# State-space step of a conv-attention hybrid: another order of its parts, split projections, masks on GpSimd

## The chip, the cores and the metric

The kernel runs on one core of a Trainium2 chip. All times are device microseconds (us) of that core; lower is better. Of the unchanged kernel three runs are given: 3096.25 us median, 3092.15 lowest, 3098.95 highest. One more execution was recorded by the hardware profiler; it took 3095.44 us, and its span from the first to the last instruction is 3093.7 us.

## What is computed

The input is four images of 128 channels and 64 x 64 pixels. A first layer (normalisation, convolutions, attention) is followed by a second one: a state-space block and a recurrence over the 4096 tokens of each image. The change lies in the state-space block, which runs once forward and once backward over the tokens. Cut to what matters:

```python
zxbcdt = x @ in_proj                                  # x: (b, 4096, 128), after a layer norm
z, xbc, dt = split(zxbcdt)
xbc = silu(causal_conv4(xbc) + conv_b)                # four taps along the tokens
xh, Bm, Cm = split(xbc)                               # 4 heads of 64, state of 64
dt = softplus(dt + dt_bias);  A = -exp(A_log)
# per chunk: Acs = cumsum(dt * A); L = exp(Acs[l] - Acs[s]) for s <= l, else 0
Y_diag = einsum('bcln,bcsn,bchls,bcshp->bclhp', Cc, Bc, L, xc)
states = einsum('bcln,bclh,bclhp->bchpn', Bc, decay_st, xc)
new    = st + carry * dec                             # the scan over chunks
Y_off  = einsum('bcln,bchpn,bclh->bclhp', Cc, prev, exp(Acs))
y  = Y_diag + Y_off + xh * D
yg = y * silu(z)
yn = yg * rsqrt(mean(yg * yg) + eps) * norm_w
return yn @ out_proj                                  # forward + reversed backward
```

All values are float32. The kernel takes chunks of 128 tokens where the reference takes 64; the result is the same function.

## The kernel before

`mamba` holds the stage. A *sequence* is one image: 32 *steps* of 128 tokens (`NT`), in eight *groups* of four steps (`NG`, `MT`). A step handles both directions at once: partitions 0 to 63 carry the forward state, 64 to 127 the backward one (`HALF`). In all there are 128 steps and 32 groups.

*The projections of a group*, for 512 columns each: `project_bc` (B or C of both directions, four taps each, two half-array products side by side, L1109), `project_fwd` (four taps, L1121), `project` (one product L1130, then ScalarE's identity with the last tap L1135, and three taps on VectorE L1141), `project_z` (L1152, Silu L1153), `outputs` (L1314). Their PSUM tiles come from `ring`, a pool of three banks, tag "big". The row statistics of other sequences (L83 to L89), which run in between, use the same ring.

*A step.* `load` fetches by DMA the cumulated decays of the chunk, spread over all partitions: `lt` (L1160, three buffers) and `ct` (L1164, two buffers). `differences` forms max(0, cs - row) for each head on ScalarE (L1174). `prepare` transposes B (`p_bt`, L1193), forms the products of B and C (`p_g`, L1195), takes Exp of the whole `lt` (L1197), copies B (L1199), weights the tokens with dt and dtd (L1202), zeroes `p_g` outside the triangle (`gm`, L1206), multiplies it into `lt` (L1207) and C into `ct` on GpSimd (L1208). `turn` transposes the tokens (L1183). `states` multiplies tokens and B (`p_st`, L1218), lets the carried state fade on GpSimd (L1227) and adds (L1230). `scan` forms y from `lt` (L1240) and from the carried state and `ct` (L1248). `take` adds the D term after every second step (L1260). `p_g`, `p_bt` and `p_st` are parts of one PSUM tile, `small`, of two banks.

*The end of a group.* `gate` multiplies with z on GpSimd (L1273), `squares` squares and adds (L1279, L1282), `means` takes the mean over channels by a product with 32 columns (L1289), adds epsilon (L1293), sends the row through DRAM into columns, takes the power -1/2 on GpSimd (L74) and spreads it back by DMA (`rs`). `back` multiplies by `rs` (L1352) and adds to the residual stream (L1355).

*Order.* Inside the stage TensorE and ScalarE run in the order of the code (`manual_schedule`); VectorE, GpSimd and SyncE, which issues the DMAs, are put in order by a scheduler from priorities and estimated times. The main loop over n does, in this order: open step n+2, states(n), turn(n+1), scan(n), prepare(n+1), take, the work of a position j = n mod 4, differences(n+2), and pieces of the opening of the next sequence and the ending of the last one. By j: 0 squares, px, pb for B, px; 1 means, px, pb for C; 2 `project_fwd`, three `activate`, all four pz, gate; 3 gate, back.

Of the kernel before, what the change touches and what calls it, by code (L numbers as in the profile page):

```python
# [16 lines left out]
P = 128  # L17
# [876 lines left out]
def mamba(nc, tc, k, a, t, B, T, vec, first=None, after=None, mr=None):  # L894
# [16 lines left out]
    with ExitStack() as ctx:  # L911
# [29 lines left out]
        mean = wp.tile([P, QT], F32, name="mean")  # L941
# [53 lines left out]
        engines = (mybir.EngineType.PE, mybir.EngineType.Activation)  # L995
        ctx.enter_context(tc.manual_schedule(engines=set(engines)))
        small = ps.tile([P, 2, NC], F32, name="small")
        p_g, p_bt, p_st = small[:, :, 0:P], small[:, 0, P : 2 * P], small[:, 1, P : P + DI]
# [5 lines left out]
        def steps(b, tl):  # L1004
# [72 lines left out]
            nc.vector.tensor_copy(flat(cs), pcs[:, 0])  # L1077
# [7 lines left out]
            pr = p_g if b == 0 else ring.tile([P, ND, P], F32, tag="big", name="pr")  # L1085
# [4 lines left out]
            nc.scalar.activation(row[:, 1], pr, AF.Exp)  # L1090
# [25 lines left out]
        def project_fwd(gr):  # L1116

            tl, g = gr["tl"], gr["at"][1]
            px = ring.tile([P, MG], F32, tag="big", name="px")
            for tap in range(KC):  # L1120
                nc.tensor.matmul(px, w[0]["x"][:, tap, :], tl[:, rows(g, 0, tap)], start=(tap == 0), stop=(tap == KC - 1))  # L1121
            nc.scalar.activation(gr["x"][0][:, 0, :], px, AF.Silu, bias=w[0]["cb"][:, 0:1])

        def project(gr, i, c):
# [5 lines left out]
            nc.tensor.matmul(px, wx, tl[:, rows(g, i, PAD)], start=True, stop=True)  # L1130
# [16 lines left out]
        def project_z(gr, i, c):  # L1147
# [4 lines left out]
            nc.tensor.matmul(pz, w[i]["z"][:, bass.ts(c, P)], tl[:, rows(g, i, PAD)], start=True, stop=True)  # L1152
            nc.scalar.activation(gr["z"][i][:, c, :], pz, AF.Silu)  # L1153

        def load(m):
# [6 lines left out]
            m["ct"] = wk.tile([P, NHEAD, P], F32, tag="ct", name="ct")  # L1162
# [6 lines left out]
        def differences(m):  # L1169

            for d in range(ND):
                for h in range(NHEAD):
                    v = m["lt"][:, d, h, :]
                    nc.scalar.activation(v, v, AF.Relu, scale=-1.0, bias=m["b"]["cs"][:, d, m["i"], h : h + 1])  # L1174

        def turn(m):
# [4 lines left out]
            for d in range(ND):  # L1181
                for c in range(2):
# [3 lines left out]
                    )  # L1186

        def prepare(m):

            gr, i = m["g"], m["i"]  # L1190
            Bs, Cs = gr["bc"][0], gr["bc"][1]
            cols = bass.ts(i % MT, P)
            nc.tensor.transpose(p_bt, Bs[:, cols], k.ident)  # L1193
            for d in range(ND):
                nc.tensor.matmul(p_g[:, d, :], Bs[HALF[d], cols], Cs[HALF[d], cols], start=True, stop=True)  # L1195
            lt = m["lt"]
            nc.scalar.activation(lt, lt, AF.Exp, scale=-1.0)  # L1197
            m["bt"] = wk.tile([P, P], F32, tag="bt", name="bt")
            nc.scalar.copy(m["bt"], p_bt)  # L1199
            for name in ("dt", "dtd"):  # L1200
                m[name] = wk.tile([P, ND, NHEAD, HD], F32, tag="x" + name, name="x" + name)
                nc.vector.tensor_tensor(  # L1202
                    m[name], m["xh"], m["b"][name][:, :, i, :].unsqueeze(3).to_broadcast([P, ND, NHEAD, HD]), ALU.mult
                )
            gm = wk.tile([P, ND, P], F32, tag="gm", name="gm")
            nc.vector.tensor_tensor(gm, p_g, k.tri, ALU.mult)  # L1206
            nc.vector.tensor_tensor(lt, lt, gm.unsqueeze(2).to_broadcast([P, ND, NHEAD, P]), ALU.mult)  # L1207
            nc.gpsimd.tensor_tensor(  # L1208
                m["ct"], m["ct"], Cs[:, cols].unsqueeze(1).to_broadcast([P, NHEAD, P]), ALU.mult
            )  # L1210

        def states(m, S):

# [8 lines left out]
            S1 = wk.tile([P, NHEAD, HD], F32, tag="S", name="S1")  # L1222
            st = p_st.rearrange("p (h c) -> p h c", c=HD)
            if S is None:
                nc.vector.tensor_copy(S1, st)
            else:
                nc.gpsimd.tensor_tensor(  # L1227
                    S1, S, m["b"]["tot"][:, i, :].unsqueeze(2).to_broadcast([P, NHEAD, HD]), ALU.mult
                )
# [3 lines left out]
        def scan(m, y, S):  # L1233

            i = m["i"]
            at = [bass.ts(i % 2, P), bass.ts(1 - i % 2, P)]
            for c in range(2):
                for d in range(ND):
                    for h in range(2):
# [3 lines left out]
                        )  # L1243
            if S is not None:
# [8 lines left out]
        def take(gr, j, y):  # L1253

            for d in range(ND):
                cols = half(d, j // 2)
                v = grp.tile([P, 2, 2 * P], F32, tag=f"y{d}", name=f"yT{d}", bufs=3)
# [11 lines left out]
        def gate(gr, j, split=False):  # L1269
            for d in range(ND):  # L1270
# [13 lines left out]
        def means(gr):  # L1284


            pm = ring.tile([ND * QT, MG], F32, tag="big", name="pm")
            for d in range(ND):
                nc.tensor.matmul(  # L1289
                    pm[bass.ts(d, QT)], mean, gr["z"][d][:, 0, :], start=True, stop=True, tile_position=(0, d * QT)  # L1290
                )
            ms = wk.tile([ND * QT, MG], F32, tag="row", name="ms", bufs=3)
# [3 lines left out]
            nc.sync.dma_start(m1.rearrange("(d q) n -> d (q n)", d=ND), ms[::QT])  # L1296
            col = wk.tile([P, n], F32, tag="col", name="col")
            nc.sync.dma_start(col, m1)
# [11 lines left out]
        def outputs(gr, d):  # L1310
            po = ring.tile([P, MG], F32, tag="big", name="po")
            for i in range(2):
                for c in range(2):
                    nc.tensor.matmul(  # L1314
                        po[:, half(d, i)], w[d]["out"][:, c, :], gr["y"][d][i][:, c, :],
                        start=(c == 0), stop=(c == 1),
                    )
# [90 lines left out]
        differences(m[0])  # L1408
        for i, c in STEPS_X:
            activate(groups[0], i, c)  # L1410
        turn(m[0])
        prepare(m[0])
        differences(m[1])
        S, y = None, None
        for n in range(N):
# [3 lines left out]
            last = g == NG - 1  # L1419
            if n + 2 < N:  # L1420
                open_step(n + 2)
            if n % NT == 0:
                S = None
            S1 = states(m[n], S)
            if n + 1 < N:
                turn(m[n + 1])
            if n % 2 == 0:
# [335 lines left out]
```

## Time and profile before

| | |
|---|---|
| runs, median (range) | 3096.25 us (3092.15 to 3098.95) |
| profiled execution, time and span | 3095.44 us, 3093.7 us |
| mean granted TensorE clock | 0.973 |
| busy share PE, DVE, ACT, POOL | 92%, 73%, 59%, 59% |
| convolution and attention, 0 to 1570 us | 1570 us |
| preparation of the state-space stage, 1570 to 1650 us | 80 us |
| state-space stage, 1650 to 2960 us | 1310 us |
| recurrence, 2960 to 3094 us | 134 us |

PE is TensorE, PEld its weight loads, DVE is VectorE, ACT ScalarE, POOL GpSimd, SP SyncE. A float32 product shows as two matmul instructions, a transpose as one. The stages are stretches of the span, told apart by the lines that run in them. The busy time of PE is an upper bound of its work, since matmuls overlap and their ends are modelled; the start of one matmul to the start of the next is the better measure of what it costs. An idle time is put down to the event that came last before the engine went on.

Some durations of the stage, each the mean of one instruction in the profile:

| line | what | ns |
|---|---|---|
| L1174 | ACT Relu of 128 x 128 (eight in a row take 2.43 us) | 390 |
| L1197 | ACT Exp of 128 x 1024 | 1057 |
| L1197, L1113, L1122 | ACT table load | 1283 |
| L1206 | DVE triangle, 128 x 256 | 416 |
| L1207 | DVE `lt` times `gm`, 128 x 1024 | 1393 |
| L1202 | DVE tokens times dt, 128 x 512, from PSUM | 684 |
| L1141 | DVE one tap, 128 x 512 | 748 |
| L1260 | DVE D term, 128 x 256 | 471 |
| L1208 | POOL `ct` times C, 128 x 512 | 1328 |
| L1273 | POOL gate, 128 x 512 | 1351 |
| L48 | POOL select, 128 x 128 (made once, in the beginning) | 300 |

### The profile page before, as it was taken

What the parts mean: (1) busy time and instruction counts of PE and PEld (TensorE: products, weight loads), DVE (VectorE), ACT (ScalarE), POOL (GpSimd) and SP (SyncE); (2) the same over time, 40 slices, a digit from 0 to 9 for tenths busy, and PEclk for the clock granted to TensorE, in tenths of its full rate; (3) what the DMA queues carried; (4) which work ended last, traced back from release to release, by engine and by line L of the source; (5) the groups of instructions that cost most, each with busy time, mean ns of one, the idle gap of its engine ahead of it and who ended that gap; (6) DMA issues with size and microseconds to landing.
All of it is one profiled execution on the core that took longest, in us unless ns stands there. A gap on an engine that the chain in (4) does not pass through costs nothing. (4 is left out here: it accounts for less than half of the span.)

```text
span 3093.7 us, 51126 instructions
## 1 busy us (share of the span) xinstructions
PE 2858.4 (92%) x19607; PEld 1461.9 (47%) x19607; DVE 2245.6 (73%) x3461; ACT 1834.4 (59%) x3134; POOL 1812.9 (59%) x1393
## 2 busy tenths in 40 slices
PE   6799999999999999999997999998999999999886
PEld 2345444454444554444463444444544444555455
DVE  6886677777787767788865767676777767676667
ACT  3253445444454444444526878876888778888756
POOL 4167458557585575876652565566556565555644
PEclk9899999999999999999998999999999999999988
DMA  5310011010100101011023343433333343333332
GB/s 185 136 39 31 24 47 34 21 44 24 47 32 23 44 24 47 28 50 44 16 81 92 90 124 86 109 88 113 96 96 92 91 103 97 100 102 101 83 111 111
DMA packets 108426, 224.68 MB, mean 73 GB/s; under 512 B 25678, under 2 KB 29390, under 8 KB 106764
## 3 DMA queue, kind: packets, MB, share of 16 engines
q1 hardware_dynamic: 96588, 177.53, 19.8%
q10 hardware_dynamic: 11584, 43.78, 4.2%
q8 instruction: 157, 2.57, 0.4%
q14 instruction: 97, 0.79, 0.1%
HBM read 200.83 MB, written 20.44 MB: 72 GB/s over the span
## 5 line engine op out<-in xcount | busy, mean ns | idle before, releaser
L480 DVE TENSOR_TENSOR es<-es,ex 128x1024 f32<-128x1024 f32 x448 | 703.0, 1569 | 83.6 <-ACT ex L463 43.2
L463 ACT ACTIVATE ex<-pf 128x1024 f32<-128x1024 f32 x512 | 497.8, 1021 | 403.8 <-PE pf L461 365.0
L461 PE MATMUL pf<-theta,phi 64*64 64x512 f32 x4096 | 496.7, 599 | 19.2 <-ACT ex L463 18.8
L473 PE MATMUL acc<-ex,gT 64*64 64x512 f32 x4096 | 486.7, 596 | 7.9 <-ACT ex L463 7.9
L1208 POOL TENSOR_TENSOR ct<-ct,Cst 128x512 f32<-128x512 f32 x128 | 170.0, 1328 | 344.0 <-DMA ct<-csmem 304.8
L1174 ACT ACTIVATE lt<-lt,cs 128x128 f32<-128x128 f32 x1024 | 312.1, 390 | 0.4 <-DMA lt<-csmem 0.4
L367 PE MATMUL pm<-yf,wt 128*128 128x256 f32 x1152 | 287.6, 382 | 15.9 <-DVE es L486 11.5
L473 PEld LDWEIGHTS acc<-ex,gT 64*64 64x64 f32 x4096 | 158.5, 135 | 298.2 <-issue 286.5
L461 PEld LDWEIGHTS pf<-theta,phi 64*64 64x64 f32 x4096 | 147.3, 133 | 311.7 <-issue 212.7
L367 PEld LDWEIGHTS pm<-yf,wt 128*128 128x128 f32 x1152 | 212.6, 189 | 99.2 <-issue 43.5
L410 ACT ACTIVATE eo<-pm 128x256 f32<-128x256 f32 x88 | 33.8, 384 | 367.6 <-PE pm L367 367.6
L1109 PE MATMUL pb<-tl,wbc_fwd 128*64 128x512 f32 x512 | 240.9, 614 | 6.9 <-DVE xT L1141 6.9
L1109 PE MATMUL pb<-tl,wbc_bwd 128*64 128x512 f32 x512 | 241.5, 615 | 0.0
L337 POOL TENSOR_TENSOR yf<-yd 128x272 f32<-128x272 f32 x192 | 230.4, 1228 | 1.4
L1273 POOL TENSOR_TENSOR yT<-yT,zT 128x512 f32<-128x512 f32 x127 | 170.9, 1351 | 57.2 <-DVE yT L1260 49.9
L1207 DVE TENSOR_TENSOR lt<-lt,gm 128x1024 f32<-128x1024 f32 x128 | 178.3, 1393 | 1.9
L337 POOL TENSOR_TENSOR yf<-xp 128x272 f32<-128x272 f32 x128 | 119.0, 961 | 97.4 <-PE pm L367 91.6
L1141 DVE SCALAR_TENSOR_TENSOR xT<-px,taps_bwd,xT 128x512 f32<-128x512 f32 x192 | 143.6, 748 | 9.7 <-ACT xT L1135 5.1
L1109 PEld LDWEIGHTS pb<-tl,wbc_fwd 128*64 128x64 f32 x512 | 66.6, 140 | 173.9 <-issue 142.1
L1240 PE MATMUL y<-lt,xdt 128*64 128x128 f32 x2048 | 141.2, 280 | 6.9 <-PE ptr L1183 4.2
L367 PE MATMUL pm<-yf,wc 128*128 128x256 f32 x512 | 133.4, 389 | 14.8 <-DVE eo L414 8.2
L1227 POOL TENSOR_TENSOR S<-S,tot 128x256 f32<-128x256 f32 x120 | 89.6, 746 | 96.1 <-PE y L1248 85.2
(299 smaller groups left out, 5714.9 us busy)
## 6 DMA issues: line engine op xcount, KB each, us to landing
lt<-csmem SPq DMA_DIRECT2D x128, 512.0 KB, 5.5
wt<-wd ACTq DMA_DIRECT2D x72, 576.0 KB, 3.7
ct<-csmem SPq DMA_DIRECT2D x256, 128.0 KB, 5.2
rs<-m SPq DMA_DIRECT2D x31, 512.0 KB, 3.7
wd<-t SPq DMA_DIRECT2D x16, 576.0 KB, 2.8
t<-in_x SPq DMA_DIRECT2D x4, 2048.0 KB, 10.7
rows<-after SPq DMA_DIRECT2D x32, 256.0 KB, 5.2
out<-t SPq DMA_DIRECT2D x4, 2048.0 KB, 14.3
```

The source lines that it names most:

```text
L337: nc.gpsimd.tensor_tensor(f[:, kx], at(x), at(y), op)
L367: nc.tensor.matmul(pm[:, e, :], wt, src, start=(i == 0), stop=(i == len(terms) - 1))
L461: nc.tensor.matmul(pf[c, e, :], phi[HALF[e], m, c], th[HALF[e]], start=True, stop=True)
L463: nc.scalar.activation(ex, pf, AF.Exp, scale=scale)
L473: nc.tensor.matmul(acc[r][HALF[e]], gT[HALF[r], 2 * m + e, :], ex[HALF[r], e, :], start=(m == 0), stop=(m == NT // 2 - 1),)
L480: nc.vector.tensor_tensor(es, es, ex, ALU.add)
L1109: nc.tensor.matmul(out, w[i]["bc"][:, tap, bass.ts(c, DS)], src, start=(tap == 0), stop=(tap == KC - 1),)
L1141: nc.vector.scalar_tensor_tensor(at(n), px, taps[:, PAD - n : KC - n], at(n), ALU.mult, ALU.add)
L1174: nc.scalar.activation(v, v, AF.Relu, scale=-1.0, bias=m["b"]["cs"][:, d, m["i"], h : h + 1])
L1207: nc.vector.tensor_tensor(lt, lt, gm.unsqueeze(2).to_broadcast([P, ND, NHEAD, P]), ALU.mult)
L1208: nc.gpsimd.tensor_tensor(m["ct"], m["ct"], Cs[:, cols].unsqueeze(1).to_broadcast([P, NHEAD, P]), ALU.mult)
L1273: eng.tensor_tensor(v, v, gr["z"][d][:, :, half(d, j // 2)], ALU.mult)
```

## The change

The parts of a step are cut anew and put in another order:

- The mask moves. `mask` puts 1e30 into `lt` outside the triangle, on GpSimd, ahead of the exponential; `gm` and its product with the triangle are gone, and `weigh` multiplies `lt` by `p_g` straight from PSUM. The cumulated sums are stored negated, and `decays` takes one Exp for each head in place of Relu, with no Exp of the whole tile after it.
- VectorE joins the engines that run in the order of the code. GpSimd and SyncE stay with the scheduler.
- `product` issues a projection as two halves of 64 output columns; `project_fwd`, `project`, `project_z` and `outputs` use it. The products of B and C (`likeness`) are four of 64 x 64 in place of two of 64 x 128, the means use 64 columns in place of 32.
- The transpose of B goes to a tile of the ring and follows the transposes of the tokens in `turn`.
- In a step: states, scan, carried state, load of step n+3, mask(n+2), `reads` and `fade` (n+1), likeness and weigh (n+1), turn and tokens (n+1), take, pieces of other sequences, work of j, decays(n+2). For at = 4 to 11 the opening's piece stands ahead of the work of j, later behind decays.
- The work of j: 0 gate of the group before, half of squares, px, pb, px; 1 other half of squares, px, pb, means; 2 `activate`, `project_fwd`, two pz, root of the means; 3 gate, two pz, gate, back.
- `ct` has three buffers (before two), `yT` four (before three).

The diff, cut to its core:

```diff
-        engines = (mybir.EngineType.PE, mybir.EngineType.Activation)
+        engines = (mybir.EngineType.PE, mybir.EngineType.Activation, mybir.EngineType.DVE)
         ctx.enter_context(tc.manual_schedule(engines=set(engines)))
         small = ps.tile([P, 2, NC], F32, name="small")
-        p_g, p_bt, p_st = small[:, :, 0:P], small[:, 0, P : 2 * P], small[:, 1, P : P + DI]
+        p_g, p_st = small[:, :, 0:P], small[:, 0, P : P + DI]
+
+        def product(out, w, src, start=True, stop=True):
+            for half in HALF:
+                nc.tensor.matmul(out[half], w[:, half], src, start=start, stop=stop)
...
-            nc.tensor.matmul(px, wx, tl[:, rows(g, i, PAD)], start=True, stop=True)
+            product(px, wx, tl[:, rows(g, i, PAD)])
...
-        def differences(m):
+        def mask(m):
+            for d, step in enumerate((-1, 1)):
+                v = m["lt"][:, d]
+                nc.gpsimd.affine_select(
+                    out=v, in_=v, compare_op=ALU.is_ge, fill=1e30, base=0,
+                    pattern=[[0, NHEAD], [-step, P]], channel_multiplier=step,
+                )
+
+        def decays(m):
             for d in range(ND):
                 for h in range(NHEAD):
                     v = m["lt"][:, d, h, :]
-                    nc.scalar.activation(v, v, AF.Relu, scale=-1.0, bias=m["b"]["cs"][:, d, m["i"], h : h + 1])
+                    nc.scalar.activation(v, v, AF.Exp, scale=-1.0, bias=m["b"]["cs"][:, d, m["i"], h : h + 1])
...
+            m["pbt"] = ring.tile([P, P], F32, tag="big", name="pbt")
+            nc.tensor.transpose(m["pbt"], gr["bc"][0][:, bass.ts(i % MT, P)], k.ident)
+
+        def likeness(m):
+            Bs, Cs = (m["g"]["bc"][c] for c in range(2))
+            at = m["i"] % MT * P
+            for h in range(2):
+                for d in range(ND):
+                    nc.tensor.matmul(
+                        p_g[HALF[h], d, :], Bs[HALF[d], ds(at + h * DS, DS)], Cs[HALF[d], ds(at, P)],
+                        start=True, stop=True,
+                    )
...
-            gm = wk.tile([P, ND, P], F32, tag="gm", name="gm")
-            nc.vector.tensor_tensor(gm, p_g, k.tri, ALU.mult)
-            nc.vector.tensor_tensor(lt, lt, gm.unsqueeze(2).to_broadcast([P, ND, NHEAD, P]), ALU.mult)
+        def weigh(m):
+            lt = m["lt"]
+            nc.vector.tensor_tensor(lt, lt, p_g.unsqueeze(2).to_broadcast([P, ND, NHEAD, P]), ALU.mult)
...
+        def fade(m, S):
+            m["S"] = None
+            if S is not None and m["i"] + 1 < NT:
+                m["S"] = wk.tile([P, NHEAD, HD], F32, tag="S", name="S1")
+                nc.gpsimd.tensor_tensor(
+                    m["S"], S, m["b"]["tot"][:, m["i"], :].unsqueeze(2).to_broadcast([P, NHEAD, HD]), ALU.mult
+                )
...
+            S1 = states(m[n])
+            if n % 2 == 0:
+                y = ps.tile([P, ND, 2, 2 * P], F32, tag="y", name="y")
+            scan(m[n], y, S)
+            carried(m.pop(n), y, S)
+            S = S1
+            if j == 0 and more:
+                open_group(G + 1)
+            if n + 3 < N:
+                open_step(n + 3)
             if n + 2 < N:
-                open_step(n + 2)
...
+                mask(m[n + 2])
+            if n + 1 < N:
+                reads(m[n + 1])
+                fade(m[n + 1], None if at == NT - 1 else S)
+                likeness(m[n + 1])
+                weigh(m[n + 1])
...
             if n + 1 < N:
                 turn(m[n + 1])
+                tokens(m[n + 1])
             if n % 2:
                 take(gr, j, y)
...
             if n + 2 < N:
-                differences(m[n + 2])
+                decays(m[n + 2])
```

## The prediction

> **What bounds the kernel now.** I read the table of stretches first, to see which engine fills the state-space stage (about 1650 to 2950 us), then the waits of that stage, then the order of time on TensorE (PE). One sequence of eight groups is the stretch below; its columns are start:end, length, then busy us (instructions) of PE, PE's weight loads, VectorE (DVE), ScalarE (ACT) and GpSimd (POOL), then granted clock, DMA share and GB/s.
>
> ```profile
> 1976.00:2302.00 326.00, 304.94 (x2108) 157.18 (x2107) 229.98 (x522) 256.14 (x510) 191.68 (x160) 0.98 0.35 97
> ```
>
> PE is busy 94% and no other engine reaches 80%; a group of four steps takes 326/8 = 40.75 us. So PE is the bound, and the question is what PE does with its time. The order of time on PE for the fixed part of one step (start, length, instruction, rows*columns of the array used):
>
> ```profile
> 2461.67 0.65 PE L1218 MATMUL small<-xdtd,bt 128*64 128x256 f32 x4
> 2462.25 0.66 PE L1183 MATMUL ptr<-ident,xT 128*128 128x128 f32 x4
> 2462.84 1.09 PE L1240 MATMUL y<-lt,xdt 128*64 128x128 f32 x16
> 2463.86 0.67 PE L1248 MATMUL y<-ct,S 64*64 64x128 f32 x16
> 2464.46 0.33 PE L1193 MATMUL small<-ident,Bst 128*128 128x128 f32 x1
> 2464.72 0.49 PE L1195 MATMUL small<-Cst,Bst 64*128 64x128 f32 x4
> 2465.14 0.70 PE L1121 MATMUL px<-tl,wx_fwd 128*128 128x512 f32 x1
> ...
> 2465.68 0.19 PEld L1121 LDWEIGHTS px<-tl,wx_fwd 128*128 128x128 f32 x1 [0.24 <-issue]
> 2466.11 0.19 PEld L1121 LDWEIGHTS px<-tl,wx_fwd 128*128 128x128 f32 x1 [0.24 <-issue]
> ```
>
> The last two rows give the pace inside a block: 0.43 us per 512 columns of the whole array, so 0.107 per 128; a half-array instruction costs half of that and a quarter a quarter, since they run side by side. Hold each block's start-to-start against this pace: L1218 0.58 for 0.43 of work, L1183 0.59 for 0.43, L1240 1.02 for 0.86, L1248 0.60 for 0.43, L1193 0.26 for 0.107, L1195 0.42 for 0.21. Each time the used shape of the array changes, 0.15 to 0.21 us are lost: 1.0 us in six changes. The order of the matmuls in a group has 6 such changes in each step (24) and 7 more among the projections (px, pb, px, next step; pm, px, pb; pz; po): 31, some 5.1 us of 40.75.
>
> The rest is real waiting. These are from the waits, the first two of PE in the stage, the third of the whole span (engine and line, what it waited for, total us, times, longest):
>
> ```profile
> PE small L1193 <- DVE S L1230: 23.5, 23, 4.2
> PEld pz L1152 <- ACT zT L1153: 34.3, 32, 1.1
> POOL ct L1208 <- DMA ct<-csmem: 304.8, 71, 8.1
> ```
>
> **The change, part by part.** *Shape changes.* With px, pz and po issued as two 64-column halves and pm as 64 columns, all projections have the shape of L1240 and L1218. A step becomes states and scan (128x64), carried and B-C products (64x64), transposes with that of B (128x128), projections (128x64): 3 changes instead of 6, none among projections, 12 per group. Gone: 3x4 at about 0.165 and 7 at 0.155 = 3.1 us a group.
>
> *Halves.* They add 38 matmul instructions a group (8 for px forward, 6 for the other px, 8 for pz, 16 for po). Nearest rows, from the chain in order of time:
>
> ```profile
> 1676.81 3.60 PE pb L1109 x16
> ...
> 1692.91 3.65 PE px L1121 x8
> ```
>
> Sixteen half-array instructions take what eight whole ones take. "TensorEngine Tiling (Array Packing)" in the Trainium skill, Instruction Overhead, speaks against it: some 60 cycles for each matmul. At the 2.4 GHz of the skill's tensor-engine page that is an estimate of 25 ns x 38 x 32 groups = 30 us lost; by the row it is zero. I take zero and keep 30 for the range.
>
> *PE's own time after.* Fixed part: 0.43 + 0.86 + 0.43 + 0.21 + 0.43 + 0.107 + 3 x 0.16 = 2.95. Projections by step: 0.86 + 3.44 + 0.86, the same with pm in place of a px, 3.44 + 1.72, 1.72 + 3.44: about 5.16 each. Together 8.11; at a clock of 0.98, 8.28; statistics transposes (16 parts of 0.43 in 32 steps) 0.22: 8.5 a step, 34.0 a group. Before, own time was 34.0 + 3.1 = 37.1, so 3.65 us of 40.75 were waiting.
>
> *Waits removed.* The pz wait (34 us, 1 a group) goes: two pz a step instead of four against three PSUM slots. S's decay on POOL is issued a step early (fade), so the S addition no longer waits for a POOL that is late. ct gets a third buffer and its load one step of lead, so POOL's 305 us go; PE never waited for them, they only make room on POOL.
>
> *Wait added: DVE in program order.* Before, the scheduler let DVE add S ahead of the last px's taps:
>
> ```profile
> 2204.38 0.78 ACT L1135 ACTIVATE xT<-px,cb_fwd,taps_fwd 128x512 f32<-128x512 f32 x1 [0.37 <-PE px L1130]
> 2205.04 0.42 DVE L1230 TENSOR_TENSOR S<-S,small 128x256 f32<-128x256 f32 x1 [0.79 <-PE small L1218]
> ...
> 2206.94 0.75 DVE L1141 SCALAR_TENSOR_TENSOR xT<-px,taps_fwd,xT 128x512 f32<-128x512 f32 x1
> ```
>
> Now the code places those taps first. Let step j=1 begin at 0, when PE has issued the last px: it ends at 0.16, ACT's identity 0.94, the three-column add and three taps (0.2 + 2.3) 3.45, S addition (0.42) 3.87. PE is through states, scan and carried at about 1.9, and the B-C product writes `small`, which the S addition reads; that PE waits for exactly this addition is in the waits above (L1193 after L1230). So it stands 2.0 us. DVE then runs weigh, two token products, take, three taps and ms (1.3 + 1.3 + 1.8 + 2.3 + 0.65), to about 12.05, while j=2 wants its product at 12.05: the S addition is 0.5 late, and 1.4 more where statistics (four at 0.28, aggregates, one scalar) stand ahead of the taps: on average 1.3. In j=2 and j=3 DVE has about 4 and 6 us: no wait. Also 0.3 at po for its PSUM slot, and 0.7 a group from the opening of the next sequence, as before. Added up: 4.3 us a group. Behind the late S addition on DVE stand weigh and the token products, whose readers are a step away.
>
> *DVE otherwise.* The triangle product gm (0.415) goes; weigh now reads PSUM: between 1.2 and 1.6, by L1202 (0.68 for half of it from PSUM) 1.3 against 1.41. DVE 228 - 13 = 215 us a sequence.
>
> *ACT.* Relu and Exp become one Exp: 8 of 0.30 stay, 1.06 a step goes. Table loads: Silu and Exp now alternate in every step, 8 a group at 1.28 against 45 in eight groups: +2.4. ACT: 256/8 - 4.2 + 3.0 = 30.8 a group. Decays now wait for POOL's mask; behind them on ACT stand the next B copy, squares and identities. Cover: their result is needed a step later.
>
> *Mask on POOL.* Two selects of 128x512 a step; the trace has only 128x128. The 4.19 us memset of 4900 and the 0.21 of 128 give 0.83 ns a column; the 0.30 select then comes to 0.62. "GPSIMD Engine Reference", Engine selection, speaks against this move (elementwise belongs on VectorE), and its section on elementwise cycle accounting has 0.77 for 512 elements in a tight loop. By the row POOL gets 5.0 a group, by the page 6.2: 29 or 30.1 of the 38 it has. I take the page, as the larger; above 1.8 us each POOL would be the bound.
>
> *Queues.* lt and ct loads three steps ahead still wait for lt's buffer, free after scan(n): SP issues them 1.5 us into the step, they land in 5.5 us, the mask needs them in the following step: hidden by about 5 us. Means moves behind the last projection of j=1 and its POOL root to j=2; back reads rs in j=3, some 8 us on; the chain of small DMAs (1.6, 2.9 and 3.7 to landing) fits barely; if late, DVE waits in back, 1 to 2 us a group.
>
> **Sum.** 34.0 + 4.3 = 38.3 against 40.75: 2.4 x 32 = 78 us, less some 8 for a stage whose first and last group gain nothing. Against the profiled 3095.4 (span 3093.7): 3025. The median of the runs is 0.8 higher, so 3026.
>
> **Rivals.** (a) *The waits vanish too*: if the B-C product doesn't wait for the S addition, only 1.0 of waiting stays: 35.0 a group, 184 us, 2912. For it: `small` is laid out anew; against: the products still span both banks of it. Chance 0.17. (b) *Slower: DVE's program order takes more than it brings.* Place: the S addition behind the step before's work. It decides from 6.7 us a group (40.75 - 34.0). If j=3 to j=0 (behind back, which waits for rs) and j=2 to j=3 also lose 2 us each on the half of groups with opening or ending work, and the j=1, j=2 waits grow by half through POOL's contention (L1207 ran from 1.23 to 2.13): 4.3 + 2 + 1.65 = 8, 1.3 x 32 = +40: 3137. For it: POOL is fuller; against: DVE has 215 busy us in 306. Chance 0.20. (c) *The halves don't run side by side*: 12.9 us of projections a group would double, +330 at least; L1109 speaks against it; 0.02. My case has 0.61.
>
> **How the numbers follow.** My case alone spans 2985 to 3075: 0 to 30 for the halves, masks of 0.62 to 0.9, a wait of 3.5 to 5.5 a group. The range 2945 to 3115 takes in half of (a) and part of (b). Within 0.2% (6 us), about what a measurement can't tell from no change, lies 0.05; faster 0.74, slower 0.21.
>
> **What would show it.** In the changed profile: no shape change inside projections, 0.16 us at three places a step; groups of about 38 us; PE waiting for the S addition at the B-C product, twice in four steps, 1 to 2 us; POOL's wait for ct gone and two selects of 0.6 to 0.9 us a step; no gm row; table loads up by about 75. Wrong, if the step's PE time isn't near 8.5 us, or if PE's longest wait names a mask, a decay or the slots.

## The result and the profile after

The changed kernel takes 3215.99 us in the median (four runs, 3212.09 to 3218.96), beside 3096.82 for the kernel before on the same chip: 1.0386 times as long, 95% interval 1.0368 to 1.0404. It is slower by 119 us, where a gain to 3026 was forecast. Its profiled execution has a span of 3217.2 us and a mean granted clock of 0.945, against 0.973.

From the page of the changed kernel, the busy times and three groups that the prediction had priced (line, operation, count, busy us, mean ns, idle time before it):

```profile
PE 2826.9 (88%) x21335; PEld 1449.7 (45%) x21335; DVE 2237.9 (70%) x3333; ACT 1811.4 (56%) x3070; POOL 1906.3 (59%) x1710
...
L1178 POOL TENSOR_SCALAR_AFFINE_SELECT lt<-lt 128x512 f32<-128x512 f32 x256 | 159.2, 636 | 445.0 <-DMA lt<-csmem 399.0
L1228 DVE TENSOR_TENSOR lt<-lt,small 128x1024 f32<-128x1024 f32 x128 | 156.3, 1221 | 237.7 <-ACT lt L1188 177.8
...
L1188 ACT ACT_TABLE_LOAD x126 | 161.7, 1283 | 2.3
```

The same stretch of 326 us as in the prediction, in the table of stretches (PE, weight loads, DVE, ACT, POOL, granted clock, DMA share, GB/s):

```profile
1976.00:2302.00 326.00, 276.48 (x2327) 143.38 (x2329) 211.91 (x459) 230.56 (x451) 204.01 (x227) 0.92 0.39 93
```

PE fell from 94% to 85% of the stretch and its clock from 0.98 to 0.92. No other engine took the place of the bound: all but GpSimd have less to do in 326 us than before, and GpSimd stands at 63%. So what was lost is lost in waiting and in the clock. The waits of the state-space stage, 1700 to 3000 us (total us, times, longest):

```profile
POOL lt L1178 <- DMA lt<-csmem: 370.4, 78, 11.1
...
DVE lt L1228 <- ACT lt L1188: 170.1, 74, 7.0
...
PEld small L1210 <- DVE S L1260: 153.9, 43, 9.4
PE small L1210 <- DVE S L1260: 143.5, 43, 9.2
```

The last line is the one to compare: PE at the B-C product, waiting for VectorE to add the state. In the window from 1700 to 2900 us, before and after:

```profile
PE small L1193 <- DVE S L1230: 23.3, 22, 4.2
PE small L1210 <- DVE S L1260: 135.7, 40, 9.2
```

The wait that the prediction named is there. It is larger than was reckoned, and it is not alone.

**An account of PE's time.** From the matmul records of steps 4 to 124 (30 groups) I split the time of a group into four parts. *Streaming* is each matmul at full clock, 0.43 us for 512 columns of the whole array; it is reckoned from the shapes, not measured. *Changes* are the places where the used shape of the array differs from that of the matmul before, at 0.155 us each, a price taken from the trace of before. *Clock* is the time in which the granted clock was at half, times a half. *Waits* is what is left, so an error in the price of a change would show up there. Us a group; "median" is of the runs.

| kernel | group | streaming | changes (number) | clock | waits | median |
|---|---|---|---|---|---|---|
| before | 40.08 | 31.78 | 5.01 (32.3) | 0.63 | 2.66 | 3096.8 |
| changed | 43.73 | 31.78 | 2.03 (13.1) | 3.47 | 6.45 | 3216.0 |

The changes of shape brought 2.98 us a group, as meant; from one shape's first matmul to the next one's, what goes beyond streaming is 0.164 us in the median before and 0.166 after, so the price holds in both kernels. Clock and waits took 2.84 and 3.79. The balance, 3.65 x 32 groups = 117 us, is the 119 that were measured.

**Where in the group.** From one step's scan to the next, in the mean: before 10.5, 10.8, 11.3 and 7.6 us for j = 0 to 3; after 10.6, 14.6, 8.6 and 10.0, with medians of 8.6, 14.7, 8.4 and 8.9. Three of four steps mostly run at the 8.1 to 8.9 us that the cut allows. This is such a stretch in the order of time on PE of the changed kernel:

```profile
2084.50 0.61 PE L1250 MATMUL small<-xdtd,bt 128*64 128x256 f32 x4
2084.93 1.05 PE L1270 MATMUL y<-lt,xdt 128*64 128x128 f32 x16
2085.91 0.67 PE L1282 MATMUL y<-ct,S 64*64 64x128 f32 x16
2086.40 0.40 PE L1210 MATMUL small<-Cst,Bst 64*64 64x128 f32 x8
2086.73 0.66 PE L1197 MATMUL ptr<-ident,xT 128*128 128x128 f32 x4
```

From start to start 0.43, 0.98, 0.49 and 0.33: each block costs its streaming and at most one change. The step j = 1 looks like this (order of time, all engines; what stands in brackets is the idle time before, and what ended it):

```profile
2116.48 0.61 PE L1250 MATMUL small<-xdtd,bt 128*64 128x256 f32 x4
...
2116.70 0.78 ACT L1140 ACTIVATE xT<-px,cb_fwd,taps_fwd 128x512 f32<-128x512 f32 x1 [0.17 <-PE px L1003]
...
2118.11 2.33 DVE L1146 SCALAR_TENSOR_TENSOR xT<-px,taps_fwd,xT 128x512 f32<-128x512 f32 x3
...
2120.35 0.41 DVE L1260 TENSOR_TENSOR S<-S,small 128x256 f32<-128x256 f32 x1
...
2120.82 0.45 PE L1210 MATMUL small<-Cst,Bst 64*64 64x128 f32 x8 [2.26 <-DVE S L1260]
...
2126.23 0.64 PE L1114 MATMUL pb<-tl,wbc_fwd 128*64 128x512 f32 x1 [2.38 <-DVE ls_st L85]
```

This is the picture that was forecast: identity, three taps, then the S addition, which starts 3.87 us after the step began (forecast: 3.45). PE stands 2.26 us where 2.0 was forecast. But it stands again at pb: the ring has three banks, and the row statistics that hold one of them now stand behind the tokens and the D term on VectorE. And this step is a mild one. Over all groups the gap before the B-C product of j = 1, in the weight loads, is 2.1 us at the tenth percentile, 3.0 in the median, 7.8 at the ninetieth and 4.0 in the mean.

The worst ones lie at steps 16, 17, 24 and 25 of an image (3.4 to 9.4 us in the three images that open another), where pieces of the next image's opening run (at step 17 of three images VectorE is also held by GpSimd; the last section shows it). VectorE of the changed kernel in such a place, step 25, and PE's B-C product behind it, in order of time:

```profile
2310.34 1.75 DVE L1053 RECIPROCAL u<-u 128x256 f32<-128x256 f32 x1 [2.89 <-ACT xe L1052]
...
2313.51 0.49 DVE L1060 TENSOR_TENSOR xe<-dt,A 128x128 f32<-128x128 f32 x2
2313.92 0.41 DVE L1260 TENSOR_TENSOR S<-S,small 128x256 f32<-128x256 f32 x1
...
2314.39 0.70 PE L1210 MATMUL small<-Cst,Bst 64*64 64x128 f32 x8 [8.49 <-DVE S L1260]
```

VectorE idles 2.89 us for ScalarE's exponential and then works off the opening's softplus. The S addition stands behind it in the order of the code, and PE waits 8.49 us for the S addition. No run gave the state products and the B-C products tiles of their own, so that the second need not wait for the addition that reads the first.

### The profile page after: what moved, and what is told of

The parts are those of the page before. It is cut to its first block, busy times and chain, and to the rows that moved or that the text cites. A ratio compares the mean times of both kernels' runs of the same rounds, so it can differ in the third digit from the quotient of the medians.

```text
span 3217.2 us, 55076 instructions
## 1 busy us (share of the span) xinstructions
PE 2826.9 (88%) x21335; PEld 1449.7 (45%) x21335; DVE 2237.9 (70%) x3333; ACT 1811.4 (56%) x3070; POOL 1906.3 (59%) x1710
## 5 line engine op out<-in xcount | busy, mean ns | idle before, releaser
L1178 POOL TENSOR_SCALAR_AFFINE_SELECT lt<-lt 128x512 f32<-128x512 f32 x256 | 159.2, 636 | 445.0 <-DMA lt<-csmem 399.0
L1228 DVE TENSOR_TENSOR lt<-lt,small 128x1024 f32<-128x1024 f32 x128 | 156.3, 1221 | 237.7 <-ACT lt L1188 177.8
L1114 PE MATMUL pb<-tl,wbc_fwd 128*64 128x512 f32 x512 | 248.3, 630 | 4.2 <-DVE ls_st L85 4.1
L1114 PE MATMUL pb<-tl,wbc_bwd 128*64 128x512 f32 x512 | 248.7, 630 | 0.0
L1233 POOL TENSOR_TENSOR ct<-ct,Cst 128x512 f32<-128x512 f32 x127 | 161.6, 1273 | 70.4 <-ACT Cst L1118 61.3
L1210 PE MATMUL small<-Cst,Bst 64*64 64x128 f32 x1024 | 59.4, 306 | 159.7 <-DVE S L1260 148.5
L1307 POOL TENSOR_TENSOR yT<-yT,zT 128x512 f32<-128x512 f32 x127 | 160.0, 1276 | 0.1
L1114 PEld LDWEIGHTS pb<-tl,wbc_fwd 128*64 128x64 f32 x512 | 76.8, 151 | 182.3 <-issue 167.0
```

The lines of the kernel that those rows point to most:

```text
L1114: nc.tensor.matmul(out, w[i]["bc"][:, tap, bass.ts(c, DS)], src, start=(tap == 0), stop=(tap == KC - 1),)
L1178: nc.gpsimd.affine_select(out=v, in_=v, compare_op=ALU.is_ge, fill=1e30, base=0, pattern=[[0, NHEAD], [-step, P]], channel_multiplier=step,)
L1228: nc.vector.tensor_tensor(lt, lt, p_g.unsqueeze(2).to_broadcast([P, ND, NHEAD, P]), ALU.mult)
L1233: nc.gpsimd.tensor_tensor(m["ct"], m["ct"], Cs.unsqueeze(1).to_broadcast([P, NHEAD, P]), ALU.mult)
L1307: eng.tensor_tensor(v, v, gr["z"][d][:, :, half(d, j // 2)], ALU.mult)
```

## The experiments

All ratios are against the kernel before (about 3095 us), with 95% intervals. Waits and clock are those of the account above, in us a group.

### VectorE back to the scheduler

```diff
-        engines = (mybir.EngineType.PE, mybir.EngineType.Activation, mybir.EngineType.DVE)
+        engines = (mybir.EngineType.PE, mybir.EngineType.Activation)
```

> The changed kernel with VectorE given back to the scheduler, nothing else. Theory T (VectorE's program order puts the S addition behind the step before's work, TensorE stands at the B-C product and its clock falls after each such stand): the wait of L1210 for the S addition falls from 155 us to under 50, the clock lost in the stage from 102 us to under 50, a group from 43.7 to 38 to 40 us, the total to 3020 to 3090. Rival D (the late thing is the chain ScalarE decays - weigh, which starves the step whatever VectorE's order is): the total stays above 3150, and TensorE waits at L1270 for weigh instead.

3107.45, 1.0040 (1.0026 to 1.0053): this one word is worth 109 of the 119 us, though the total stays above the 3020 to 3090 that theory T gave. Waits 4.95 and clock 1.93, against 6.45 and 3.47. In PE's waits, 1700 to 2900 us, the S addition falls from 135.7 to 32.7 us, but banks held by late taps come in:

```profile
PE small L1210 <- DVE S L1260: 32.7, 22, 7.0
PE px L1003 <- DVE xT L1146: 26.9, 10, 8.1
PE pb L1114 <- DVE xT L1146: 21.1, 14, 3.6
```

It does not get below before, so the 3 us of shape changes are given back even without VectorE's fixed order. That leaves a second question.

### The kernel before, with VectorE in the order of its code

```diff
-        engines = (mybir.EngineType.PE, mybir.EngineType.Activation)
+        engines = (mybir.EngineType.PE, mybir.EngineType.Activation, mybir.EngineType.DVE)
```

> The kernel before with only VectorE put in the order of the code. Theory T: the S addition comes behind the last taps here too, TensorE waits for it at the transpose of B (L1193) in j=1, 2 us or more a group plus the clock: 3150 to 3230. Rival O (program order alone is harmless, the new order of the step makes the wait): 3090 to 3110.

3209.11, 1.0359 (1.0331 to 1.0387). On the old order, with nothing else changed, the fixed order costs about as much as the whole change does: waits 5.01 (from 2.66), clock 2.10 (from 0.63). The line is the same wait as in the changed kernel, in this kernel's names, PE alone, 1700 to 2900 us; it was 23.3 us in the kernel before:

```profile
PE small L1193 <- DVE S L1230: 101.1, 45, 6.3
```

### The S addition ahead of the last taps

The taps of the last px of j = 0 are issued behind the next step's states.

```diff
+            while held:
+                held.pop()()
...
-                    project(groups[G + 1], *STEPS_X[1])
+                    project(groups[G + 1], *STEPS_X[1], held)
```

> The changed kernel in VectorE's program order, with only the taps of the last px of position 0 moved behind the S addition of the next step. Theory T: the wait at the B-C product in j=1 falls from a mean of 4.0 us to 1 to 2, a group loses 2 to 4 us with the clock's part, the total comes to 3080 to 3150. Rival D (decays late): the total stays within 1% of 3216, since weigh and all behind it start as late as before.

3178.43, 1.0263 (1.0236 to 1.0290): 38 us better than the changed kernel. The gap before the B-C product of j = 1 falls from 4.0 to 2.3 us, yet the step only from 14.6 to 14.1: the taps now hold their bank longer (PE waits 17.5 us for them at px, where the changed kernel has no such wait). The total lies between the two readings. One repaired place is a third of the cost of the fixed order. PE still waits 92.2 us for the S addition, most of it at j = 1 (2.3 us a group) and j = 0 (1.0).

### Only the halves

The kernel before, with all projections as two halves of 64 columns and the means with 64 columns.

```diff
-            nc.tensor.matmul(px, wx, tl[:, rows(g, i, PAD)], start=True, stop=True)
+            product(px, wx, tl[:, rows(g, i, PAD)])
...
```

> The kernel before with only the projections in halves of 64 columns and the means in 64 columns; order, masks and VectorE's scheduler as before. Theory P (each change of the array's used shape costs 0.155 us; 31 changes a group become 24, and halves cost nothing): 7 x 0.155 x 32 = 35 us less, 3050 to 3075. Rival C (each added matmul instruction costs 25 ns or more): 38 x 32 x 25 ns = 30 us more than that, 3085 to 3130.

3084.63, 0.9961 (0.9946 to 0.9976). The total lies at the edge of rival C's range, but the pace speaks against it: from its first matmul to that of the next block `project_fwd` takes 3.49 us as sixteen halves, and 3.54 as eight whole products with a change of shape behind them; the forward pz takes 1.72 in both forms. So the 30 us of instruction overhead that the prediction kept for its range do not show here. Changes fall from 32.3 to 27.8 a group, 0.70 us or 22 in all; waits take back 0.4 a group, and 10 us are left.

### One projection moved from j = 1 to j = 2

The changed kernel with the scheduler's VectorE; px(1,1) is issued a step later, its Silu at the end of that step.

> The changed kernel with VectorE left to the scheduler and the px of (1, 1) with its taps moved from position 1 to position 2. Theory V (with the shape changes gone a step needs 8.5 us of TensorE, and VectorE has some 18 us of work in positions 0 and 1, so TensorE waits there for PSUM slots that the taps hold): the step after j=1 falls from 13.3 to 10 to 11 us, a group from 40.7 to 38 to 39, the total to 3030 to 3070. Rival (the slots are held by B's transposes in the ring, not by taps): no more than 15 us gained, 3090 to 3110.

3117.31, 1.0079 (1.0062 to 1.0096). The step of j = 1 gains, 13.3 to 12.0 us, and j = 2 loses as much, 8.6 to 9.7. Waits go up to 5.61: PE waits 37.0 us at the means for GpSimd's sums, which it did for 2.1 before. Nothing is gained over 3107.45, so evening out VectorE's work in j = 1 is no cure, and what the S addition and the taps no longer hold up, the means do.

The same move and half of z put into j = 3, on the kernel before with halves:

> The order of before with halves, and the same evening out: px of (1, 1) to position 2, the backward pz to position 3 with both gates. Theory V: the pz wait (34 us) and the tap waits (18 us) go, and the halves' 35 us come out in full: 3030 to 3065. Rival: position 3 is now as long as the others, and nothing is gained over the 3085 of halves alone: 3075 to 3100.

3087.32, 0.9976 (0.9966 to 0.9986), the same as the halves alone within their intervals. The steps are evener (9.0, 10.4, 10.6 and 9.8 us), which brings nothing by itself.

### The decays ahead of the work of a step

VectorE waits 170 us at `weigh` for decays that ScalarE reaches only behind the last projection's identity. Here they stand in front of the work of j.

```diff
+            if n + 2 < N:
+                decays(m[n + 2])
...
-            if n + 2 < N:
-                decays(m[n + 2])
```

> The changed kernel, VectorE in program order, with only decays(n+2) on ScalarE moved ahead of the work of j instead of behind it. Rival D (weigh, in VectorE's order, stands for decays that come at the end of the step before; all behind it starts late, the S addition with it): weigh's wait for ScalarE falls from 170 to under 60 us and the total by 60 to 110 us, to 3105 to 3155. Theory T alone (only the taps ahead of the S addition are the cause): within 1% of 3216, or slower, since the px identities now come later.

3319.44, 1.0727 (1.0709 to 1.0745), over 100 us worse; waits 9.2, clock 4.3, the step of j = 1 at 17.0 us. The wait of `weigh` for the decays is gone from the list, as rival D meant, and yet the kernel is slower. ScalarE now stands longer at the copy of B, for PE's transpose, and VectorE stands for the identities of the projections, which come behind the decays. Of the kernel's waits, 1700 to 2900 us (the changed kernel has 170.4 and 42.6 there):

```profile
ACT bt L1218 <- PE pbt L1202: 378.8, 80, 11.3
...
DVE xT L1144 <- ACT xT L1140: 122.7, 46, 3.9
```

With the taps of the last px held back as well, so that the S addition goes first:

> Both edits in VectorE's program order: decays ahead of the work of j, and the last taps of position 0 behind the next S addition. T and D together: about the sum of the two, 3070 to 3120, near what the scheduler's order gave (3107). If something else in program order holds VectorE (back's wait for rs, the opening's chain): 3140 to 3180.

3231.61, 1.0432 (1.0415 to 1.0450), above both readings: holding the taps back brings 88 us here and 38 above, so much of the loss in this order is again the S addition behind the taps; the rest was not taken apart. That the decays come late is a symptom, and putting them first is no cure.

### Halves, with the transposes first

The kernel before with halves; the transposes of tokens and of B stand ahead of the states, and the B-C products are four of 64 x 64. VectorE and GpSimd are the scheduler's, the mask is before's.

```diff
+            nc.tensor.transpose(p_bt, gr["bc"][0][:, bass.ts(i % MT, P)], k.ident)
...
+            if n + 1 < N:
+                turn(m[n + 1])
             S1 = states(m[n], S)
-            if n + 1 < N:
-                turn(m[n + 1])
```

> The kernel before with the halved projections and means, and now also the transposes of tokens and of B ahead of the states, and the B-C products as four of 64x64: changes of the array's shape fall from 27.8 to about 20 a group, VectorE and GpSimd stay in the scheduler's order and the mask stays where it was. Theory 'shape changes are worth 0.155 us each wherever they go': about 1.2 us a group less than with the halves alone (3084.6), so 3045 to 3055. Theory 'the step's order decides, the gain is swallowed by waits of TensorE for ScalarE's or VectorE's results': 3075 to 3090 or worse, with the waits per group above 3.1 us.

3061.85, **0.9883** (0.9863 to 0.9902): the fastest of all that ran, 1.2% below before. Changes 16.5 a group, so 2.45 us are gained, of which waits take 1.52 (4.18); the clock stays at 0.51. A group takes 39.03, 1.05 less than before, which over 32 groups is the 34 us measured. Both theories have a part: the changes bring what they were priced at, and waits take more than half of it back (PE for the S addition 42.2 us and for taps at pb 26.6, against 23.3 and 6.9 before).

### The mask taken off GpSimd again

The changed kernel with the scheduler's VectorE; Relu in the decays, one Exp of the tile, and the triangle multiplied into the B-C products in PSUM by VectorE.

```diff
-                nc.gpsimd.affine_select(
-                    out=v, in_=v, compare_op=ALU.is_ge, fill=1e30, base=0, ...
...
+            nc.scalar.activation(lt, lt, AF.Exp, scale=-1.0)
+            nc.vector.tensor_tensor(p_g, p_g, k.tri, ALU.mult)
```

> The changed kernel with VectorE back with the scheduler (3107.5), and the mask on GpSimd undone: Relu in the decays, one Exp of the whole tile and the triangle multiplied into the B-C products in PSUM by VectorE. Theory 'GpSimd, which stands at the mask until the decay rows land, holds gate, fade and the sums of squares behind it, and TensorE's waits come from there': 3060 to 3085, waits per group from 4.95 down to about 3.5. Theory 'the new order of the step itself makes the waits, the mask only happens to be where GpSimd is idle': 3100 to 3120, since ScalarE has 4 us a group more to do.

3090.33, 0.9987 (0.9973 to 1.0001), between the two theories: moving the mask to GpSimd, with all that the move spares ScalarE and VectorE, costs about 17 us net. It shows in the clock (1.93 to 0.97); waits stay at 4.91. They have other names now. The S addition has fallen from 32.7 to 13.3 us, and at the top of PE's waits, 1700 to 2900 us, stand banks of the ring:

```profile
PE pz L1003 <- ACT bt L1215: 25.2, 17, 2.1
PE px L1003 <- DVE xT L1146: 19.9, 11, 4.1
```

The first comes of the changed cut: B's transpose lies in the ring, so a bank waits until ScalarE has copied it. The changed kernel has 6.8 us of it and the kernel before none. How the mask on GpSimd costs its 17 us was not taken apart.

### The transposes behind the B-C products

As "halves, with the transposes first", but with the order of products that the changed kernel has in a step.

```diff
-            turn(m[n + 1])
             S1 = states(m[n], S)
...
+            turn(m)
             lt = m["lt"]
```

> The kernel with halves and early transposes (3061.9) with the transposes of tokens and of B behind the B-C products instead of ahead of the states: the order of a step's products is then that of the changed kernel, while the group's work is cut and placed as before, the mask is before's and VectorE is the scheduler's. Changes of shape 16.5 to about 13 a group, 0.55 us a group or 17 us. Theory 'the changed order of a step is sound, what the changed kernel loses with the scheduler's VectorE lies in its cut of the group's work and in the mask': 3040 to 3060. Theory 'tokens and B copy turned so late make the states wait': 3075 to 3100, as the kernel without the mask (3090).

3089.48, 0.9982 (0.9973 to 0.9990), 28 us slower than with the transposes first. Both readings missed in part. Changes of shape are 15.9 a group, hardly below 16.5: row statistics, which are transposes too, now stand between projections and states and need two changes of their own. And waits are 4.88, not 4.18. Tokens turned this late leave VectorE waiting for them (waits, 1700 to 2900 us; 92.2 us with the transposes first), and PE waits at the scan without a releaser that the profile names (6.1 us with the transposes first). How much of the 28 us each of these makes was not measured:

```profile
DVE xdt L1212 <- PE ptr L1188: 117.0, 79, 5.8
...
PE y L1250 <- issue: 24.4, 15, 2.6
```

### Useless work in the gap

The changed kernel; in each step j = 1, 16 transposes that nobody reads stand ahead of the B-C product.

```diff
+                if j == 1:
+                    keep_busy(m[n + 1])
                 likeness(m[n + 1])
```

> The changed kernel with work added that nobody needs: in each step j=1, right ahead of the B-C product, TensorE transposes the same tokens four times more (16 transposes, 1.71 us, and two more changes of shape, about 2.0 us a group), into the tile that the transposes behind it overwrite. The B-C product still waits for the S addition, 4.0 us in the mean without the filler. Theory 'a TensorE that stands for over 2 us loses clock in the 3 to 10 us after': the filler takes the place of idling, windows at half clock fall from about 35 to 15 or 20 in 1700 to 2900 us, the time lost to them from 3.5 to about 2 us a group, and the kernel gets faster by 20 to 50 us in spite of the work: 3165 to 3195. Theory 'the clock has other causes, or the wait only moves with the filler': 3215 to 3260.

3196.78, 1.0334 (1.0304 to 1.0363): 19 us *faster* than the changed kernel, with 1.74 us more streaming and two more changes a group. The gap before the product of j = 1 falls from 4.0 to 2.1 us and the clock term from 3.47 to 2.16. In the order of time on PE of this kernel, the filler and the product behind it:

```profile
2105.37 1.97 PE L1210 MATMUL ptr<-ident,xT 128*128 128x128 f32 x16
2107.77 0.45 PE L1221 MATMUL small<-Cst,Bst 64*64 64x128 f32 x8 [0.43 <-DVE S L1271]
```

Streaming, changes and waits together rise by 0.46 us a group (the filler is a little longer than the waiting it replaces); the clock term falls by 1.31 and decides the sign. The gain falls just short of the 20 to 50 us expected. The lost clock is thereby a cost of its own, on top of the wait that brings it on.

## Why the prediction was wrong

The mechanism was that of rival (b), VectorE's program order, which had a chance of 0.20, and its size was three times that reckoned there: +119, not +40 us. My case named the same wait, PE at the B-C product for the S addition, and priced it too low, and that is the step that failed: 3.3 us a group in the sum (2.0 at j = 1 and 1.3 at j = 2), 5.8 measured (4.0, 0.28, and 1.55 at j = 0), and behind the waits 2.8 us of clock that the sum had held fixed. Of rival (b)'s further places, j = 0 lost time and j = 3 none. By the prediction's own steps:

- **Shape changes: right.** 31 to 12 was forecast, 3.1 us a group; counted 32.3 to 13.1, 2.98.
- **Halves: right.** No cost: 3.49 us for sixteen halves, 3.54 for eight whole products and a change.
- **The base, 40.75 us a group: 0.7 too long.** 326 us are not quite one image's eight groups; counted from step 4 to 124 a group took 40.08. Over 32 groups this makes the forecast gain some 21 us too large, and explains none of the loss.
- **PE's own time, 34.0 us a group: it failed in one term, the clock at 0.98.** Streaming and changes come to 33.81. At the clock that was held fixed this is 34.5, but the clock fell: 3.47 us a group were lost to it, where 0.98 of 34.0 allows 0.7. This term is 2.8 of the 5.4 us by which a group came out above 38.3; the waits below are 2.15, and 0.5 is own time that was reckoned too low. A wait was priced at its length alone.
- **"Wait added: DVE in program order", 4.3 us a group with the small ones: mis-sized.** Measured 6.45. The 2.0 us at j = 1 is what an undisturbed group shows (2.26 in the step above, 2.1 at the tenth percentile); the mean is 4.0. Two things were left out. The opening and statistics pieces were counted at j = 2 with 1.4 us, but they sit before j = 0 and j = 1 too, where PE waits up to 9.4 us (j = 0: 1.55 us in the mean, forecast none; j = 2: 0.28, forecast 1.3). The 1.3 rests on a sum that does not come out: 3.87 and the five items listed make 11.2 us, not 12.05, and so VectorE in time for j = 2. And in a fixed order VectorE does not only run late, it waits itself: for ScalarE's exponential (2.89 us in the rows above), for `rs` (24.2 us, 1700 to 2900), for the decays at `weigh`.
- **"Cover: their result is needed a step later": wrong.** The decays of step n+2 are issued at the end of step n, ScalarE starts them behind the last identity, and VectorE wants them at `weigh` early in step n+1: 170 us of waiting. But the decays' place was not the root; put first they cost more.
- **Mask: the row was right.** 0.636 us a select, 0.62 by the row; the larger figure I took, 0.77, was too high. GpSimd never became the bound, yet the mask's move cost about 17 us net in the kernel with the scheduler's VectorE, which the prediction had at nothing.
- **`weigh`** took 1.22 us (1.3 forecast), table loads rose by 64 (75 forecast).
- **"For it: POOL is fuller; against: DVE has 215 busy us in 306".** This was the argument that set the chance of (b), and it was the wrong kind. Busy share says nothing about an engine in fixed order that is needed within two us of each step. The kernel before with a fixed VectorE order, 3.6% slower on an unchanged load, shows it.
- **Waits removed: they moved, and the freed PE time did not stay.** GpSimd's wait for `ct` falls from 304.8 to 8.7 us (1650 to 2960), but it stands 375.8 us for `lt` at the mask, which the prediction had hidden by 5 us. The weight loads of pz wait 11.7 us for z in place of 34.3, but those of po wait 28.0, where the kernel before has no such line. And the program order is not all: it costs 3.03 us a group (43.73 against 40.70 with the scheduler's VectorE), not more than the 3.3 reckoned, yet without this wait the sum has 35.0 and the run 40.70: with the S addition out of the way, other waits come forth, 4.95 us a group in all against 2.66 before and the 1.0 of the sum. What takes the gain differs by the cut: banks of the ring held by taps, B's transpose in the ring, tokens turned late, GpSimd at the mask. With the transposes first and the rest left alone, 1.05 of the 2.45 us gained stay. Which share belongs to each in the changed kernel was not taken apart further.

## What to carry to other kernels

Before an engine is put in program order, list for each of its results that the bound engine waits for, what stands ahead of it in the code, in the worst group and not the mean one; the scheduler's freedom was worth 3.6% here on an unchanged kernel. Price a wait of TensorE above its length: those of over 2 us mostly cost clock too. And take a change of order apart first: here the halves, the quartered B-C products and transposes grouped ahead of the states gave 1.2% by themselves, while the whole cost 3.9%.

## What the runs showed of the hardware

**Clock after a wait.** Three stretches of the changed kernel around the second wait of the step shown above (start:end, length, PE busy, granted clock, DMA share, GB/s):

```profile
2123.20:2126.20 3.00, 0.65 (x4) 1.00 0.09 29
2126.80:2130.20 3.40, 3.40 (x12) 0.51 0.00 0
2130.60:2134.00 3.40, 3.40 (x42) 1.00 0.00 0
```

PE idled 2.38 us; some 0.6 us after it had resumed, the clock fell to half for 3.4 us. All such windows in the stage are about 3.4 us long, or two to four times that. In the changed kernel 34 of them begin between 1700 and 2900 us (before: 7), and 32 begin within 4 us of an idle stretch of over 2 us. Over all fourteen kernels, idle stretches of PE from 1700 to 2900 us by length, and how many had a half-clock window begin within 4 us of their end:

| idle, us | 1 to 1.5 | 1.5 to 2 | 2 to 2.5 | 2.5 to 3.5 | over 3.5 |
|---|---|---|---|---|---|
| stretches | 189 | 131 | 117 | 53 | 121 |
| with a window | 9 | 35 | 66 | 38 | 120 |

The Trainium skill ("TensorE: Matmul & The Clock Gate", What's actually happening) tells of a free-running window of about 3.4 us and a half-rate state after an idle one. The lengths agree; but here more than half of the gaps of 2 to 2.5 us were already followed by it. The share differs from kernel to kernel (8 of 9 in the one with useless work, none of 9 in the one without the mask), so the length of a gap alone does not settle it.

**VectorE held by GpSimd.** The three-column add between neighbouring groups takes 0.15 us at least and 0.22 in the median, but once it took 7.36. Of the changed kernel, in order of time, the add, the last of nine GpSimd instructions that ran without a pause, and VectorE's next instruction:

```profile
2206.57 7.36 DVE L1144 TENSOR_TENSOR xT<-xT,xT 128x3 f32<-128x3 f32 x1 [1.28 <-ACT xT L1140]
...
2212.65 1.26 POOL L1233 TENSOR_TENSOR ct<-ct,Cst 128x512 f32<-128x512 f32 x1
...
2214.03 2.33 DVE L1146 SCALAR_TENSOR_TENSOR xT<-px,taps_bwd,xT 128x512 f32<-128x512 f32 x3
```

The add ends at 2213.93, GpSimd's run at 2213.91. Each of the 23 such adds of over 0.9 us in the stage ends within 0.05 us after the end of a GpSimd instruction. "SBUF — State Buffer" of the Trainium skill (SBUF: two separate sides) has the two engines share a pair of ports that one holds for a whole instruction; here the hold seems to have passed over a chain of GpSimd instructions. What all these adds took beyond 0.156 us sums to 45 us over the stage (7.5 in the kernel before, 37 with the scheduler's VectorE). The three of over 4 us stand ahead of the S addition of step 17 of three images, where PE then waited 5.8 to 7.3 us for it. No run took this out.
